# A transformer block with a mixture of experts on one core: the slots' first layer computed transposed, the routing weights from the tokens' side, eight groups in place of five, and another order of work at the start

## The chip, the cores and the metric

The kernel runs on one core of a Trainium2 chip. The metric is device time in microseconds (us) for one execution, as the median of several runs. TensorE is written PE (its weight loads PEld), VectorE DVE, ScalarE ACT, GpSimd POOL, SyncE SP.

## The reference

The input is `x`, 16 batches of 512 tokens with 128 features. Cut to what matters:

```
mod = silu(c) @ wmod                       # per batch: sa, ca, ga, sb, cb, gb
h = layernorm(x) * (1 + ca) + sa
x = x + ga * attention(h)                  # 16 heads of 8, rope, causal mask, softmax, proj
h = layernorm(x) * (1 + cb) + sb           # hidden state of a token
probs = sigmoid(h @ router_w.T + bias)     # 160 experts
top_w, top = top_k(probs, 8);  top_w = 2.5 * top_w / sum(top_w)
routed = sum over the 8 chosen e of top_w[e] * (silu(h @ w_gate[e].T) @ w_down[e].T)
shared = silu(h @ w_gate_shared.T) @ w_down_shared.T
out = x + gb * (routed + shared)
```

Each expert has 64 inner features, so two experts make a pair of 128, and there are 80 pairs. 8192 tokens with 8 choices each are 65536 rows to be sent through an expert.

## The kernel before, in words

**Two stages.** The attention stage goes through 16 batches times 4 groups of 4 heads, 64 passes of `attend(gg, pacer)`. The later stage, called the slots' stage below, sends the chosen rows through the experts. The order on PE, SP, ACT and DVE is written out by hand. A small clock in the program (`Steps`, `Pacer`) counts the modelled time of the matmuls issued so far and decides where background work is put between them; nothing of that clock exists at run time.

**Attention.** `prepare(b)` normalises a batch, and `rotate` and `values` make its queries, keys and values. Queries and keys go to DRAM (`parts`) and come back spread over 96 rows (`fetch`, tiles `qrep`, `krep`). `maxima` takes the row maxima of the scores on DVE, `shift` puts them into `qrep` through a DMA (`qrep<-mT`), `exponentials` runs on ACT, and `weighted` multiplies by the values. `project` adds the result to `x`. `route` then computes hidden states and the eight choices of a batch. Both run as background steps inside later passes.

**Groups, blocks, quads.** The batches are cut into `GROUPS = (4, 4, 4, 3, 1)`. When the last batch of a group is routed, `place(gr)` gives every chosen row a slot: slots are sorted by pair of experts, each pair takes whole blocks of 128 slots, at least one. A group of n batches is given 32n + 80 blocks, since up to 80 blocks can be partly full. Four blocks are a quad. The last 8 quads of a group (6 in a group of one batch) are spare: `spare_quads` holds their code under a runtime branch. The quads that always run are 44, 44, 44, 36 and 22, in sum 190.

**Scatter and gather.** POOL sends rows of hidden states to their slots with indirect DMAs (`scattering`, `xg<-hs,idx`, 128 rows each, 512 in all), a batch after its group is placed. Before that the slots are set to zero (`clear`, `xg<-zeros`, 256 KB each, from SP): after 5 of the 14 items of each attention pass one clear is issued, and what is left over is issued after the last pass. The rows of spare quads in `yg` are cleared in the same list. After a group's last quad POOL fetches the results (`gathering`, `got<-yg,idx`, 512 in all), eight for a block of 128 tokens, and `combine` adds the eight up on DVE, and scales them. `Pacer(PACE_SLOTS, scatter, gather)` with PACE_SLOTS = 0.9 places one indirect DMA per 0.9 us of modelled time, scatters first. `add_up(LAG)` with LAG = 4 keeps at most four fetched blocks waiting before DVE is told to combine one.

**A quad.** The loop over `i` runs one stage for each of several quads:

```
("load", i + 3), ("load_down", i - 3), ("name_up", i - 1), ("name_down", i - 5),
("end_weights", i - 4), ("begin_weights", i - 3),
("turn", i), ("up", i - 2), ("back", i - 4), ("down", i - 6),
```

`load` reads 512 slots' rows (`xs<-xg`, 256 KB), `load_down` the second layer's weights (`wd<-in_wdT`, 256 KB, address from a register). `turn` transposes the rows on PE (four 128x128 f32), and ACT copies them to `xT`. `up` multiplies with `xT` as the stationary operand and the pair's weights `wg[:, pid]` as the moving one, 130 columns: 128 for the two experts, and two router columns, from which DVE and ACT compute the slot's weight (`begin_weights`, `end_weights`, in pairs of quads). A bf16 matmul with `away` adds -1e30 where a slot belongs to the other expert of the pair. ACT applies silu (`su`). Because the slots now lie on partitions, `back` transposes again on PE, and DVE copies to `hwT`. `down` multiplies by `wd`, DVE scales by the weight into `y`, and SP stores it (`yg<-y`, 256 KB). `shared_expert(b)` computes the shared expert of a batch as background steps through one PSUM bank `o`.

**The start.** `modulation` and the bias parts are computed first, inside a scratch pool. Only then are the attention's pool and its constants made (`ident`, `wqk`, `turn`, ...). DVE clears the first pair of `qrep`/`krep`, POOL the others and the value tiles. All constants (`load_rest` too) are loaded before the first `prepare`, and the first pass waits in the program until batch 1 is prepared.

Of the kernel before, what the change touches and what calls it, by code (L numbers as in the profile page):

```python
# [9 lines left out]
FP = mybir.dt.float32  # L10
BF = mybir.dt.bfloat16
I32 = mybir.dt.int32
# [23 lines left out]
GROUPS = (4, 4, 4, 3, 1)  # L36
TOPK = 8
FAR = 1e30
TINY = 1e-30
LAG = 4  # L40

PACE, PACE_SLOTS = 1.3, 0.9
# [28 lines left out]
def block_kernel(ctx: ExitStack, tc: tile.TileContext, t: dict, out: bass.AP):  # L71
# [49 lines left out]
    fetch_x(0)  # L121
    with tc.tile_pool(name="pmod", bufs=1, space=PSUM) as pp, tc.tile_pool(
        name="smod", bufs=1
    ) as sp:
        mod = modulation(nc, t, const, pp, sp)
# [9 lines left out]

        bias3 = const.tile([3, E], BF, tag="bias3", name="bias3")
        three_ = sp.tile([1, 3, E], BF)
# [3 lines left out]
        nc.vector.tensor_tensor(three_[:, 2, :], bias_e, three_[:, 1, :], ALU.subtract)  # L141
        for i in range(3):
            nc.sync.dma_start(out=bias3[i : i + 1, :], in_=three_[:, i, :])
    attn = ExitStack()
    sa = attn.enter_context(tc.tile_pool(name="attn", bufs=1))
    now.ps = attn.enter_context(tc.tile_pool(name="attn_ps", bufs=1, space=PSUM))
    c = SimpleNamespace(
        ident=load("ident", [P, P]),
        wqk=load("wqk", [D, 2, 2, D], pool=sa),
        bqk=load("bqk", [D, 2, 2], pool=sa),  # L150
        turn=load("turn", [D, 2, S], pool=sa),
        wv=load("wvT", [D, D], pool=sa),
        identb=load("identb", [P, P], BF),
        mask_q=load("mask_q", [P, 2, P], BF, pool=sa),
        mask_k=load("mask_k", [P, 2, P], BF, pool=sa),
        wproj=wproj,
        onesb=load("onesb", [P, P], BF),
    )

    def load_rest():  # L160
        c.wrout = load("wroutT", [D, E])
        c.wgs = load("wgsT", [D, I])
        c.wds = load("wdsT", [I, D])
        c.bias_p = load("bias_p", [NC, 2])
        c.ones = load("ones", [P, 1])
        c.earlier = load("earlier", [P, P], BF)
        c.many = load("many", [1, P], BF)
        c.pairs = load("pairs", [NC, 2, NC])
        c.spread = load("spread", [NC, 2, E])
        c.table = load("table", [P, 2, NKM])  # L170

    eps = const.tile([P, 1], FP, tag="eps", name="eps")
    nc.vector.memset(eps, EPS)
    minus = const.tile([P, 1], FP, tag="minus", name="minus")
    nc.vector.memset(minus, -1.0)
    zeros = const.tile([P, 2, D], FP, tag="zeros", name="zeros")
    nc.vector.memset(zeros, 0.0)
# [6 lines left out]

    stat = const.tile([P, 2, NB * NBLK, 2], FP, tag="stat", name="stat")

    def moments(kind, b, blocks):
        for j in blocks:  # L190
            six = sb.tile([P, 6], FP, tag="six", name="six", bufs=2)
            vec.bn_stats(six, xs[b][:, j, :])
            vec.bn_aggr(stat[:, kind, b * NBLK + j, :], six)
# [46 lines left out]
    reps = []  # L240
    for i in range(NREP):
        pair = [
            sa.tile([P, GH, S], BF, tag=f"{side_}rep{i}", name=f"{side_}rep{i}") for side_ in "qk"
        ]
        for rep in pair:
            (in_order(nc.gpsimd.memset(rep, 0.0).ins) if i else nc.vector.memset(rep, 0.0))
        ones_ = pair[1][MROW : MROW + 3]
        (in_order(nc.gpsimd.memset(ones_, 1.0).ins) if i else nc.vector.memset(ones_, 1.0))
        reps.append(pair)

    vs = [sa.tile([P, NBLK, VW], FP, tag=f"v{i}", name=f"v{i}") for i in range(3)]
    for v in vs:
        in_order(nc.gpsimd.memset(v, 0.0).ins)
        in_order(nc.gpsimd.memset(heads_of(v)[:, :, :, HD : HD + 1], 1.0).ins)
# [5 lines left out]
    def prepare(b):  # L260

        for j in range(0, NBLK, 2):
            moments(0, b, (j, j + 1))
            yield
# [222 lines left out]
    rows = [tc.dram_tile([P, NBLK, D], FP, name=f"rows{b}") for b in range(NB)]  # L487

    somes = const.tile([1, len(GROUPS)], I32, tag="somes", name="somes")

    class Group:
        def __init__(self, g):
# [4 lines left out]
            self.scale = sb.tile([P, self.tb], FP, tag=f"scale{g}", name="scale")  # L497
            self.idx = sb.tile([P, self.tb, TOPK], I32, tag=f"idx{g}", name="idx")
            self.shift = sb.tile([P, self.nk, 2], FP, tag=f"shift{g}", name="shift")
            self.pid = sb.tile([1, self.nq, 9], I32, tag=f"pid{g}", name="pid")  # L500
            self.some = somes[:, g : g + 1]
            self.away = sb.tile(
                [P, -(-2 * self.nk // P), P], BF, tag=f"away{g}", name="away"
            )
            self.m, self.before = [], []
            self.xg = tc.dram_tile([self.nk * P, D], FP, name=f"xg{g}")
# [13 lines left out]
    def route(gr, i):  # L520
# [40 lines left out]
        yield  # L561

        top = sb.tile([P, NBLK, TOPK], FP, tag="top", name="top")
        for j in range(NBLK):
            vec.max(top[:, j, :], key[:, j, :])
            vec.match_replace(
                out=key[:, j, :], in_to_replace=top[:, j, :], in_values=key[:, j, :], imm_value=1.0
# [4 lines left out]
        vec.tensor_scalar(m, key, 0.0, None, ALU.is_gt)  # L572
# [13 lines left out]
        yield  # L586

        rs = gr.scale[:, i * NBLK : (i + 1) * NBLK]
        vec.reciprocal(top, top)
        vec.tensor_reduce(rs, top, AX.X, ALU.add, negate=True)  # L590
        vec.tensor_scalar(rs, rs, TOPK_EPS, None, ALU.add)
        vec.reciprocal(rs, rs)
        vec.tensor_scalar(rs, rs, ROUTED, None, ALU.mult)

    def place(gr):
# [41 lines left out]

# [58 lines left out]
        lim = gr.shift[:, :nk, :]  # L696
# [715 lines left out]
```

## Time and profile before

| | |
|---|---|
| median of 3 runs | 1918.97 us (1918.86 to 1922.9) |
| profiled execution, its own time | 1925.86 us |
| its span (first to last instruction) | 1924.1 us |
| busy: PE, DVE, ACT, POOL | 1584, 1254, 827, 1118 us |
| mean granted PE clock | 0.934 |
| moved by DMA | 377 MB, mean 196 GB/s |

In the profile a stretch of time ("window") is given with each engine's busy time, the granted PE clock and the DMA engines' busy share. A group line reads: line of the source, engine, operation, out<-in, count, then total busy and mean ns of one, then the idle time ahead of them and what ended it. An f32 matmul counts as two instructions here (two passes).

### The profile page before, as it was taken

What the parts mean: (1) busy time and instruction counts of PE and PEld (TensorE: products, weight loads), DVE (VectorE), ACT (ScalarE), POOL (GpSimd) and SP (SyncE); (2) the same over time, 40 slices, a digit from 0 to 9 for tenths busy, and PEclk for the clock granted to TensorE, in tenths of its full rate; (3) what the DMA queues carried; (4) which work ended last, traced back from release to release, by engine and by line L of the source; (5) the groups of instructions that cost most, each with busy time, mean ns of one, the idle gap of its engine ahead of it and who ended that gap; (6) DMA issues with size and microseconds to landing.
All of it is one profiled execution on the core that took longest, in us unless ns stands there. A gap on an engine that the chain in (4) does not pass through costs nothing. (4 is left out here: it accounts for less than half of the span.)

```text
span 1924.1 us, 38397 instructions
## 1 busy us (share of the span) xinstructions
PE 1584.2 (82%) x12683; PEld 1133.7 (59%) x12747; DVE 1253.8 (65%) x3325; ACT 826.6 (43%) x1366; POOL 1117.9 (58%) x1139
## 2 busy tenths in 40 slices
PE   2799999998999989999888887888898878878700
PEld 1355555554555545555468776777788777777600
DVE  2677888887788867787636554546576656666622
ACT  1366666655666556664544332333233323323100
POOL 4001111047775477845657476777777777777776
PEclk8799999998999999999999898999899989999855
DMA  2456555565676667843257676778688878878622
GB/s 83 105 175 201 170 174 170 163 197 177 191 234 188 199 192 219 262 127 117 77 185 244 197 251 203 240 246 275 214 266 272 258 225 272 255 251 254 196 58 57
DMA packets 246678, 377.03 MB, mean 196 GB/s; under 512 B 37604, under 2 KB 136261, under 8 KB 246469
## 3 DMA queue, kind: packets, MB, share of 16 engines
q1 hardware_dynamic: 213700, 307.17, 51.4%
q0 software_dynamic: 32768, 67.17, 12.1%
q8 instruction: 119, 1.95, 0.4%
q14 instruction: 91, 0.74, 0.1%
HBM read 195.15 MB, written 178.26 MB: 194 GB/s over the span
## 5 line engine op out<-in xcount | busy, mean ns | idle before, releaser
L741 POOL DMA_INDIRECT xg<-hs,idx x512 | 493.4, 964 | 284.5 <-issue 95.0
L950 POOL DMA_INDIRECT got<-yg,idx x512 | 491.5, 960 | 156.7 <-issue 123.5
L1212 DVE TENSOR_REDUCE mins<-s 128x2 f32<-128x1024 f32 (+3 forms) x448 | 395.9, 913 | 123.5 <-PE s L104 121.7
L1212 ACT ACTIVATE pT<-s 128x1024 f32<-128x1024 f32 x320 | 323.0, 1021 | 176.7 <-PE s L104 172.3
L104 PE MATMUL s<-wg,xT 128*128 x1520 | 279.6, 307 | 0.6 <-issue 0.6
L104 PEld LDWEIGHTS s<-wg,xT 128*128 128x128 f32 x1520 | 241.6, 200 | 11.3 <-issue 1.2
L111 PE MATMUL turn<-ident,xs 128*128 128x128 f32 x760 | 123.8, 287 | 121.8 <-issue 49.7
L104 PE MATMUL s<-krep,qrep 96*128 96x512 bf16 (+3 forms) x1024 | 197.8, 306 | 31.9 <-DMA qrep<-parts 19.0
L104 PE MATMUL down<-wd,hwT 128*128 x1520 | 206.6, 280 | 3.7 <-DVE y L1212 3.7
L235 POOL TENSOR_TENSOR rot<-rot,three 128x512 f32<-128x512 f32 x32 | 36.8, 1160 | 291.4 <-ACT three L1212 289.4
L104 PE MATMUL s<-qrep,krep 128*128 128x128 bf16 (+3 forms) x960 | 181.6, 299 | 25.3 <-DVE mins L1212 12.3
L104 PE MATMUL av<-pT,v 128*32 128x512 f32 (+3 forms) x2048 | 193.4, 449 | 0.0
L104 PEld LDWEIGHTS down<-wd,hwT 128*128 128x128 f32 x1520 | 190.8, 197 | 4.1 <-DVE y L1212 4.0
L1212 ACT COPY xT<-turn 128x512 f32<-128x512 f32 x190 | 109.8, 578 | 164.8 <-PE turn L111 161.8
L111 PEld LDWEIGHTS turn<-ident,xs 128*128 128x128 f32 x760 | 85.6, 145 | 156.8 <-issue 116.4
L1212 DVE TENSOR_TENSOR z<-s,shift 128x8 f32<-128x8 f32 x190 | 29.6, 156 | 219.3 <-PE s L104 206.5
L104 PEld LDWEIGHTS <-identb 128*128 128x128 bf16 x1280 | 122.0, 100 | 84.9 <-issue 7.0
L104 PE MATMUL s<-identb,away 128*128 128x128 bf16 (+1 forms) x760 | 171.2, 225 | 0.0
L1212 ACT ACTIVATE su<-s 128x512 f32<-128x512 f32 x190 | 113.6, 598 | 129.3 <-DVE z L1212 121.8
L1212 DVE COPY hwT<-back 128x512 f32<-128x512 f32 x190 | 131.0, 689 | 44.2 <-PE back L111 43.6
L1212 DVE TENSOR_TENSOR y<-down,w 128x512 f32<-128x512 f32 x190 | 131.2, 691 | 38.5 <-PE down L104 33.6
L104 PEld LDWEIGHTS <-qrep 96*128 96x128 bf16 x1024 | 83.6, 99 | 119.7 <-issue 95.5
(179 smaller groups left out, 2356.6 us busy)
## 6 DMA issues: line engine op xcount, KB each, us to landing
xg<-zeros SPq DMA_DIRECT2D x228, 256.0 KB
xs<-xg SPq DMA_DIRECT2D x190, 256.0 KB
wd<-in_wdT SPq DMA_DIRECT2D x190, 256.0 KB
yg<-y SPq DMA_DIRECT2D x190, 256.0 KB
krep<-parts SPq DMA_DIRECT2D x64, 288.0 KB
qrep<-parts SPq DMA_DIRECT2D x192, 96.0 KB
parts<-three SPq DMA_DIRECT2D x96, 128.0 KB
yg<-zeros SPq DMA_DIRECT2D x38, 256.0 KB
```

The source lines that it names most:

```text
L104: steps.last = nc.tensor.matmul(out_, lhsT=lhsT, rhs=rhs, start=start, stop=stop).ins
L111: steps.last = nc.tensor.transpose(out_, in_, ident).ins
L235: in_order(getattr(nc.gpsimd, op)(*args).ins)
L741: s = nc.gpsimd.indirect_dma_start(out=gr.xg, out_offset=bass.IndirectOffsetOnAxis(ap=gr.idx[:, NBLK * i + j, k : k + 1], axis=0), in_=h[: ...
L950: s = nc.gpsimd.indirect_dma_start(out=got[:, k, :], out_offset=None, in_=gr.yg, in_offset=bass.IndirectOffsetOnAxis(ap=gr.idx[:, NBLK * i ...
L1212: return getattr(self.engine, op)(*args, **kwargs)
```

## The change

- `GROUPS = (2, 3, 3, 2, 2, 2, 1, 1)`, LAG = 3, PACE_SLOTS = 0.75. The quads that always run are 28, 36, 36, 28, 28, 28, 22 and 22, in sum 228; the blocks to clear rise from 228 quads plus 38 spare ones to 288 plus 60.
- `up` is transposed: the pair's weights are stationary. Since these are chosen at run time, ACT and DVE copy two of the four blocks each from `wg` to a fixed tile `wq` (`fetch_up`, addresses read into registers of ACT and DVE). The result has the inner features on partitions, so `back` and the copy `hwT` go away, and silu's output feeds `down`.
- The mask (`away`, four bf16 matmuls a quad) becomes one bf16 matmul of two rows, `half` by `hide`. `hide` is made in `place`, goes to DRAM, and is loaded for two quads at once (`load_hide`).
- The slot's weight is no longer computed. ACT copies the second layer's result to `y` unscaled. `route` stores the keys and the mask of choices of each batch to DRAM (`keys`, `chosen`), a new background step `weights(b)` loads them in the slots' stage and picks the eight weights of each token in slot order, and `combine` multiplies the eight rows by them.
- The quad's pipeline is two stages shorter. PSUM gets two buffers each for `turn` and `up`, and one pair of banks `s`.
- At the start the moments of batch 0 come first on DVE, `load_first` loads what `prepare(0)` needs right behind `wmod`, POOL clears the tiles (two pairs first, the rest behind `prepare(0)`), `load_rest` comes after the first four fetches, and the first pass no longer waits for batch 1.

```diff
-GROUPS = (4, 4, 4, 3, 1)
+GROUPS = (2, 3, 3, 2, 2, 2, 1, 1)
-LAG = 4
+LAG = 3
-PACE, PACE_SLOTS = 1.3, 0.9
+PACE, PACE_SLOTS = 1.3, 0.75
...
+    moments(0, 0, range(NBLK))
...
+        mod = modulation(nc, t, const, pp, sp, load_first)
...
+    clear_v(0)
+    clear_rep(0)
+    clear_rep(1)
...
+        nc.sync.dma_start(out=keys[b], in_=key)
...
+        nc.sync.dma_start(out=chosen[b], in_=m)
...
+            hide = sb.tile([P, P], BF, tag="hide", name="hide", bufs=2)
+            vec.tensor_copy(hide[:k], pa[:k, n * P : (n + 1) * P])
+            for a in range(2):
+                nc.sync.dma_start(
+                    out=gr.hide[a, c0 * I : (c0 + k) * I].rearrange("(n s) -> n s", s=P),
+                    in_=hide[a:k:2],
+                )
...
+        def load_hide(self):
+            if self.q % 2 == 0:
+                two = moe.sb.tile([2, 2, S], BF, tag="hides", name="hides", bufs=3)
+                at = slice(4 * P * self.q, 4 * P * (self.q + 2))
+                nc.sync.dma_start(
+                    out=two, in_=self.gr.hide[:, at].rearrange("a (n s) -> a n s", s=S)
+                )
+                self.hide, self.other.hide = two[:, 0, :], two[:, 1, :]
...
+        def fetch_up(self):
+            self.wq = self.tile([P, 4, P], "wq", 3)
+            for engine, copy, at in (
+                (mybir.EngineType.Activation, act.copy, 0),
+                (mybir.EngineType.DVE, vec.tensor_copy, 2),
+            ):
+                for j, pid in enumerate(self.numbers(engine, 1 + at, 2, NC - 1), at):
+                    copy(
+                        self.wq[:, j, :], wg[:, bass.ds(pid, 1), :].rearrange("p o n -> p (o n)")
+                    )
...
         def up(self):
-            pu = bank2().rearrange("p a (j n) -> p (a j) n", j=2)
+            pu = now.ps.tile([P, S], FP, tag="up", name="up", bufs=2)
             for j in range(4):
+                to = pu[:, j * P : (j + 1) * P]
                 mm(
-                    pu[:, j, 0 : P + 2],
+                    to,
+                    self.wq[:, j, :],
                     self.xT[:, j * P : (j + 1) * P],
-                    wg[:, bass.ds(self.pids[j], 1), :].rearrange("p o n -> p (o n)"),
...
+            mm(pu, c.half, self.hide, False, True)
+            self.u = self.tile([P, S], "su", 3)
+            act.activation(self.u, pu, AF.Silu)
...
-        def back(self):
-            pt = now.ps.tile([P, S], FP, tag="back", name="back")
-            for j in range(4):
-                turned(pt[:, j * P : (j + 1) * P], self.u[:, j, :], c.ident)
-            self.hT = self.tile([P, S], "hwT", 3)
-            vec.tensor_copy(self.hT, pt)
...
-                    self.hT[:, j * P : (j + 1) * P],
+                    self.u[:, j * P : (j + 1) * P],
...
-            vec.tensor_tensor(
-                y,
-                py.rearrange("p (n d) -> p n d", d=D),
-                self.w[:, self.q % 2].unsqueeze(2).broadcast_to([P, 4, D]),
-                ALU.mult,
-            )
+            act.copy(y.rearrange("p n d -> p (n d)"), py)
...
+    def weights(b):
+        while len(weighed) < weighing.index(b):
+            yield
+        key = moe.sb.tile([P, NBLK, E], FP, tag="wkey", name="wkey")
+        nc.sync.dma_start(out=key, in_=keys[b])
+        m = moe.sb.tile([P, NBLK, E], BF, tag="wm", name="wm")
+        nc.sync.dma_start(out=m, in_=chosen[b])
+        yield LATER
+        base = moe.sb.tile([P, NBLK, E], FP, tag="base", name="base")
+        vec.tensor_tensor(base, m, c.high.unsqueeze(1).broadcast_to([P, NBLK, E]), ALU.mult)
...
+        for n, (by, mask) in enumerate(((16, 0x7FFF), (0, 0xFFFF))):
+            vec.tensor_scalar(digit, bits, by, mask, ALU.logical_shift_right, ALU.bitwise_and)
+            vec.tensor_tensor(both, base, digit, ALU.add)
+            yield
+            for j in range(NBLK):
+                vec.max(eight[:, n, j, :], both[:, j, :])
...
+        vec.tensor_tensor(
+            got, got, w[:, j, :].unsqueeze(2).broadcast_to([P, TOPK, D]), ALU.mult
+        )
         for n in (4, 2, 1):
...
     for i in range(-3, len(quads) + 5):
+            ("load_hide", i),
+            ("load_down", i - 1),
+            ("fetch_up", i),
...
+            ("name_down", i - 3),
+            ("down", i - 4),
```

## The prediction

> **What bounds the kernel now.** I read the page's slices, then busy time by windows set at the stages' borders. The windows' columns: length, busy PE, PEld, DVE, ACT, POOL (instructions), granted PE clock, DMA share, GB/s.
>
> ```profile
> PE   2799999998999989999888887888898878878700
> POOL 4001111047775477845657476777777777777776
> DMA  2456555565676667843257676778688878878622
> ```
> ```profile
> 0.00:77.00 77.00, 31.15 (x113) 17.41 (x114) 29.57 (x76) 12.71 (x24) 23.13 (x23) 0.80 0.31 79
> 77.00:972.00 895.00, 841.59 (x6809) 468.50 (x6871) 695.51 (x1693) 540.61 (x792) 408.48 (x403) 0.98 0.59 177
> 972.00:1260.00 288.00, 239.10 (x1940) 216.43 (x1941) 150.91 (x499) 99.17 (x192) 188.35 (x196) 0.94 0.71 225
> 1260.00:1816.00 556.00, 467.27 (x3812) 428.55 (x3810) 351.74 (x998) 172.93 (x358) 421.90 (x439) 0.96 0.81 253
> 1816.00:1924.00 108.00, 5.12 (x14) 2.78 (x14) 26.08 (x63) 1.18 (x2) 76.06 (x81) 0.50 0.24 62
> ```
>
> A start of 77 us with PE 40% busy; attention to 972 us, PE 94% busy; the quads' loop from the first `turn` at 974 to 1816 us, 842 us or 4.43 for each of 190 quads, PE 84% busy, DMA 0.71 to 0.81; a tail of 108 us with POOL alone. From 1260 us POOL's 439 instructions in 556 us are one per 1.27 us, an indirect DMA (0.96) and its gap (0.30): POOL is full to the end.
>
> ```profile
> L741 POOL DMA_INDIRECT xg<-hs,idx x512 | 493.4, 964 | 284.5 <-issue 95.0
> L950 POOL DMA_INDIRECT got<-yg,idx x512 | 491.5, 960 | 156.7 <-issue 123.5
> ```
>
> One undisturbed quad in PE's timeline (start, length):
>
> ```profile
> 1597.99 0.66 PE L111 MATMUL turn<-ident,xs 128*128 128x128 f32 x4 [0.97 <-ACT xT L1212]
> 1598.49 0.39 PE L104 MATMUL s<-wg,xT 128*128 x2
> ...
> 1599.77 0.61 PE L111 MATMUL back<-ident,su 128*128 128x128 f32 x4
> 1600.22 1.06 PE L104 MATMUL down<-wd,hwT 128*128 x8
> 1601.11 0.60 PE L111 MATMUL turn<-ident,xs 128*128 128x128 f32 x4
> ```
>
> From start to start: `turn` 0.50, `up` with masks 1.28, `back` 0.45, `down` 0.89, in sum 3.12 us. The rest of 4.43 is the shared expert, the clock (0.95), waits for `xs` and the groups' ends, where PE branches over the spare code:
>
> ```profile
> L896 PEldq COMPARE_BRANCH  x5: 3787/5002/5340, 1185.7 to 1814.5; - x5
> ```
>
> **The start: -10 us (-18 to -3).** Batch 0's statistics waited behind tile clears, though `cT`, loaded after `x`, was there at 3.9 us:
>
> ```profile
> 19.36 0.29 DVE L1212 BATCH_NORM_STATS2 six<-x 128x6 f32<-128x128 f32 x1
> ```
>
> After the change they come first, and the next bound on DVE is the modulation and bias work, which ended at 12.5 us. ACT's normalisation then starts near 13 instead of 21.9: 9 us. POOL's clears ahead of its first subtraction are two pairs and one value tile, 6 x 1.80 + 0.87 = 12 us, done before they are needed; the other two pairs stand behind that subtraction (near 29 us), and end before 45, about when their fetch is reached. The first pass stood at 77.1 us behind batch 1's 9 us of matmuls (68.2 to 77.1). Without that wait it starts earlier, but those matmuls move into a stage that is 94% PE, so I count 1 us.
>
> **Attention: +5 us (0 to +14).** Eight placings instead of five; by 972 us about 5.6 are done instead of 2.6. One costs PE some 4.5 us (the 160-column f32 matmuls 1.2, four of 0.3 over the blocks, transposes 0.7, the rest small). Three are 13.5 us, against 53 us in which PE idles here. `hide` goes through SP with two buffers and three pieces, so DVE's third copy waits for the first piece's stores, 2 to 3 us a group, and the `maxima` queue behind it; three score buffers cover most. The routing's five weight steps go.
>
> **Clears: +8 us (0 to +18).** 64 passes issue 320 of 348 clears. With the last passes' own, 35 stand in a row on SP between the last `qrep<-mT` (957 us before) and the first `xs`: 35 x 262 KB is 9.2 MB, 29 us at the highest rate that I found:
>
> ```profile
> 1140.00:1150.00 10.00, 7.96 (x73) 7.57 (x72) 4.20 (x13) 2.91 (x7) 7.63 (x8) 1.00 0.99 322
> ```
>
> The remaining attention covers 14 us. Of the other 15 some return, since the first three `turn`s of before took 5.6 us to come.
>
> **The quads' loop: +3 us (-65 to +75).** 228 quads, 38 more. By the reference's choices for these inputs no spare quad runs, before or after. The floor of each engine:
> - PE: 0.50 + 0.89 (`up` now has `down`'s shape) + 0.25 for the mask (one bf16 pass of 512 columns; an f32 one of two passes is 0.62) + 0.89 = 2.53 us. 228 x 2.53 = 577; the shared expert 16 x 3.3 = 53; placings 15; by clock 0.95: 679. Seven groups' ends inside the loop (four before) at 6.5 us, 4.3 idle and the rest at a lowered clock: 45. Floor 724, with 2% for what I overlook 740.
> - ACT: `xT` 0.58, `su` 0.60, `y` 0.58, two copies like `gate` 0.27, and a register load, on ACT 0.28 to 0.76 in the branch's rows, 0.48: 2.8 us, 635.
> - DVE loses `hwT`, `y` and the weight steps (2.0 us a quad), and gets two copies (below 0.30, the 128x128 addition) and a load of 0.31, 0.9 x 228 = 205; the product over 128x1024, twice the 0.68 of 128x512 less its fixed part, 1.25 x 64 = 80; `weights`, 0.83 + 2 x (0.51 + 0.83) + 8 x 0.32 + 10 x 0.2 = 8 us x 16 = 131. Little more than before, and `wq` is asked for two quads ahead.
> - POOL: in program order 370 scatters come before the loop (314 before), and 485 gathers are placed within it (453). Gathers begin after 28 quads, some 105 us; then 64 scatters and 480 gathers at 1.255 us take 683: 788.
> - DMA: before, 288 us at 225 and 556 at 253 GB/s are 205 MB. Added: 38 quads x 0.786 = 30 MB, keys and choices 8, gathers 3, scatters -4, `hides` 1: 244 MB. A share of 0.81 at 253 and 0.71 at 225 means 315 GB/s when full: 775 us.
>
> So the longest floor passes from PE to DMA. Lookahead is three quads, as before, so a late transfer is mostly met by others already queued; I take 3% loss, 800 us. Add 31 for seven groups' ends, in which SP stands 4.5 us, and 15 for the stretch of quads 64 to 128: there 96 gathers are placed in 22 quads, 120 us of POOL against 78 of quads; LAG 3 lets POOL be 24 gathers, 30 us, behind, so 12 are left, once or twice. DVE then waits for `got`, behind it `wq`'s copies, and PE for those. Sum 845. The low end is PE's 740 with 37 of waits, the high end is the first rival.
>
> A row speaks against the new DVE copies: POOL's DMAs take 0.94, but one of those that ran beside DVE's additions took 0.2 more.
>
> ```profile
> 1801.51 1.47 DVE L1212 TENSOR_TENSOR got<-got 128x512 f32<-128x512 f32 x3
> 1802.33 1.14 POOL L950 DMA_INDIRECT got<-yg,idx  x1 [0.30 <-issue]
> ```
>
> Its mean over all is 0.96, so I add nothing. [...]
>
> **The tail: -55 us (-62 to -45).** 81 POOL instructions follow 1816 us, because gathers trail the quads. After the change the group before the last is fetched while the last one's 22 quads run, so 32 remain: 32 x 1.255 = 40, before it `y`, its landing and the branch 5, after it landing 2.6, combining 1.25 + 2.1, the store 2.5: 53.
>
> **Sum.** -10 + 5 + 8 + 3 - 55 = -49. The profiled execution took 1925.86 us (span 1924.1), so its like would take 1877; the median of the runs is 6.9 lower, so 1870.
>
> **The rivals.**
> - DMA becomes the bound and stays below its peak. For: the best 25 us windows of before reach 280 and 284 GB/s; 10 us at 322 is short. Against: in those windows PE was 92 to 95% busy and DMA not asked for more. At 284: 244 MB take 859 us, with 31 + 27 for groups' ends and waits 917, +75: 1870 + 72, about 1942. It decides when the rate between groups' ends falls under some 289 GB/s (a loop of 894 us). Chance 0.24.
> - DMA hides, and PE's floor rules: a loop of 777 us, 1870 - 68 = 1802, but POOL's 788 and the 40 us of tail hold it near 1815. For: without gathers a quad needs 0.88 MB, 2.8 us. Against: gathers run beside most quads. Chance 0.14.
> - The copies only change their engine: each register load stands open on ACT for 1.0 us, PE's median for such loads, and `y` and `xT` queue behind it. 3.4 us a quad with waits of 0.3 are 844, with 31 + 15: 890, +45: 1912. For: ACT's order is fixed. Against: on PE these loads delayed hardly a matmul. Chance 0.11.
>
> **How the numbers follow.** The forecast (1840 to 1900) has 0.51. 0.2%, 4 us, is about what a measurement of this kernel can tell from no change. Faster: 0.51 + 0.14 and more than half of the ACT case, 0.72; same 0.04; slower 0.24. For 8 in 10 the range takes most of the fast case and half of the slow one's upper side: 1820 to 1947.
>
> **What would show it.** Right: the first `six` near 4 us and the first pass near 60; DMA's share at 0.9 or more in the loop; a quad at 3.7 us; fewer than 40 gathers after the last `down`. Wrong: a loop with DMA still at 0.8 while ACT or DVE hold PE up, POOL's DMA above 1.0 us in the mean, or DVE waiting for `got` in the loop by more than 40 us.

## The result, and the profile after

The changed kernel takes 2000.76 us in the median of four runs (1994.59 to 2006.29), the kernel before 1918.91 on the same chip: a ratio of 1.042, 95% interval 1.039 to 1.046. The forecast was 1870 us with a range of 1820 to 1947. The kernel became slower instead of faster, and slower than the slowest rival said (1942).

The profiled execution has a span of 1998.5 us, 74.4 more than before. First the same three rows of its page (40 slices), then busy time by windows at the new borders of the stages, with the columns of before.

```profile
PE   3799998999899988889959788887777789888880
POOL 5101117713775567775726757677777774757736
DMA  3365646756766676767688688887787888888871
```
```profile
60.00:1002.00 942.00, 860.70 (x6933) 471.94 (x6931) 703.44 (x1693) 544.04 (x798) 463.72 (x458) 0.98 0.64 197
1002.00:1024.00 22.00, 0.27 (x2) 0.30 (x3) 1.10 (x7) 1.08 (x3) 0.96 (x1) 0.56 1.02 331
1024.00:1945.00 921.00, 768.74 (x5227) 644.02 (x5225) 440.86 (x1358) 526.03 (x1212) 628.52 (x625) 0.90 0.82 265
1945.00:1998.50 53.50, 0.22 (x2) 0.02 (x1) 14.86 (x29) 0.59 (x1) 30.24 (x32) 0.52 0.21 59
```

Attention now ends at 1002 us instead of 971. Then TensorE stands for 22 us while the DMA engines are full (a share of 1.02, 331 GB/s) with the clears left over. The loop of 228 quads takes 921 us, 79 more than that of 190, at a granted clock of 0.90 (0.94 to 0.96 before) and a DMA share of 0.82. The tail is 53.5 us instead of 108. So the change adds 31 us by attention's end, the start included, then 19 and 79, and takes 55 off the tail: 74 us more.

GpSimd's two groups, to be set beside those of before, and an undisturbed stretch of TensorE's timeline (start, length):

```profile
L968 POOL DMA_INDIRECT got<-yg,idx x512 | 514.6, 1005 | 240.0 <-issue 120.3 <-SPq L868 45.7 <-PE turn L110 22.1
L746 POOL DMA_INDIRECT xg<-hs,idx x512 | 499.0, 975 | 325.5 <-PE s L103 124.8 <-issue 92.2 <-PE turn L110 26.2
```
```profile
1928.07 0.60 PE L110 MATMUL turn<-ident,xs 128*128 128x128 f32 x4
1928.50 1.06 PE L103 MATMUL up<-xT,wq 128*128 128x128 f32 x8
1929.49 0.39 PE L103 MATMUL up<-hides,half 2*128 2x512 bf16 x1
1929.81 1.16 PE L103 MATMUL down<-wd,su 128*128 x8
1930.80 0.60 PE L110 MATMUL turn<-ident,xs 128*128 128x128 f32 x4
```

From one `turn` to the next are 2.73 us: `turn` 0.43, `up` 0.99, the masks 0.32, `down` 0.99. That is the quad of the change, 0.4 us under the 3.12 of before. But the mean over the loop is 921 / 228 = 4.04 us. The difference stands in single waits of several microseconds. Those of the loop, on TensorE and VectorE (total, times, longest):

```profile
PE o L110 <- DMA hr<-rows: 33.1, 7, 6.7
PE up L103 <- DVE wq L1227: 28.0, 14, 6.0
PE up L103 <- DMA hides<-hide: 24.2, 13, 2.9
DVE got L1227 <- DMA got<-yg,idx: 64.8, 22, 5.7
```

One such place in full, from the timelines of TensorE, VectorE, SyncE and GpSimd:

```profile
1425.15 1.23 PE L103 MATMUL up<-xT,wq 128*128 128x128 f32 x4 [3.67 <-DVE wq L1227]
1428.24 0.58 PE L103 MATMUL up<-hides,half 2*128 2x512 bf16 x1 [1.87 <-DMA hides<-hide]
1420.97 1.23 DVE L1227 TENSOR_TENSOR got<-got,w 128x1024 f32<-128x1024 f32 x1 [2.86 <-DMA got<-yg,idx]
1424.40 0.39 SPq L992 DMA_DIRECT2D out<-xr  x1
1425.39 0.33 SPq L800 DMA_DIRECT2D hides<-hide  x1
1422.15 0.95 POOL L968 DMA_INDIRECT got<-yg,idx  x1 [0.30 <-issue]
1423.40 0.94 POOL L968 DMA_INDIRECT got<-yg,idx  x1 [0.30 <-issue]
```

VectorE waits for gathered rows, sums them to 1424.4, and only then copies two weights of the next quad: TensorE has waited 3.67 us for them. The output's store waits for that sum too, and the masks' load stands behind the store in SyncE's order, so TensorE waits again. Beside all this GpSimd issues one gather per 1.25 us, without a break.

### The profile page after: what moved, and what is told of

The parts are those of the page before. It is cut to its first block, busy times and chain, and to the rows that moved or that the text cites. A ratio compares the mean times of both kernels' runs of the same rounds, so it can differ in the third digit from the quotient of the medians.

```text
span 1998.5 us, 39212 instructions
## 1 busy us (share of the span) xinstructions
PE 1652.7 (83%) x12248; PEld 1129.4 (57%) x12248; DVE 1185.2 (59%) x3150; ACT 1081.0 (54%) x2031; POOL 1151.8 (58%) x1142
## 3 DMA queue, kind: packets, MB, share of 16 engines
q1 hardware_dynamic: 265152, 375.32, 58.6%
## 5 line engine op out<-in xcount | busy, mean ns | idle before, releaser
L968 POOL DMA_INDIRECT got<-yg,idx x512 | 514.6, 1005 | 240.0 <-issue 120.3
L103 PE MATMUL down<-wd,su 128*128 x1824 | 279.7, 299 | 33.9 <-ACT su L1227 9.7
L103 PEld LDWEIGHTS down<-wd,su 128*128 128x128 f32 x1824 | 235.3, 202 | 116.4 <-issue 47.4
L103 PE MATMUL up<-xT,wq 128*128 128x128 f32 x1824 | 267.0, 292 | 34.2 <-DVE wq L1227 28.0
L103 PEld LDWEIGHTS up<-xT,wq 128*128 128x128 f32 x1824 | 245.2, 208 | 37.7 <-DVE wq L1227 30.9
L1227 DVE COPY wq<-wg 128x128 f32 x456 | 89.9, 244 | 243.9 <-PE up L103 163.7
L1227 ACT COPY y<-down 128x512 f32<-128x512 f32 x228 | 133.9, 587 | 182.9 <-PE down L103 126.4
L103 PE MATMUL s<-qrep,krep 128*128 128x512 bf16 (+3 forms) x1024 | 195.2, 303 | 32.6 <-DMA qrep<-mT 12.0
L1227 ACT ACTIVATE su<-up 128x512 f32<-128x512 f32 x228 | 136.4, 598 | 103.7 <-PE up L103 102.8
L1227 DVE TENSOR_TENSOR got<-got,w 128x1024 f32<-128x1024 f32 x64 | 78.3, 1223 | 102.1 <-DMA got<-yg,idx 99.0
L1227 ACT COPY wq<-wg 128x128 f32 x456 | 113.6, 296 | 42.3 <-issue 12.5
```

The source lines that it names most:

```text
L103: steps.last = nc.tensor.matmul(out_, lhsT=lhsT, rhs=rhs, start=start, stop=stop).ins
L968: s = nc.gpsimd.indirect_dma_start(out=got[:, k, :], out_offset=None, in_=gr.yg, in_offset=bass.IndirectOffsetOnAxis(ap=gr.idx[:, NBLK * i ...
L1227: return getattr(self.engine, op)(*args, **kwargs)
```

## The experiments

The experiments ran on chips that differ. On one, in this document the slower chip, the kernel before takes some 2200 us (the sets that begin with a_groups5, a_again and b_nogot); on the others, the faster chips, some 1920. Each ratio is to the kernel before on the same chip. The one trace of the kernel before is of a faster chip.

**Groups, quad, DMA volume, early loads (the slower chip, 2198 us).** Theory A says that the eight groups cost the time, B that the transposed quad's new waits do.

a_groups5: the change with the groups of before.
```
-GROUPS = (2, 3, 3, 2, 2, 2, 1, 1)
+GROUPS = (4, 4, 4, 3, 1)
```


> The changed kernel with the five groups of before, (4, 4, 4, 3, 1): 190 quads instead of 228, five placings, 266 clears; everything else as changed. Theory 1, the number of groups is the price: attention ends near 972 us again instead of 1002 (three placings fewer before that), the first turn follows within 3 us instead of 22 (no clears left over), the loop falls from 921 us to about 770 with its 38 quads gone, the tail grows from 53 to about 100 us because gathers trail again: in sum about 1850 us. Theory 2, the new quad is the price (copies of the weights on ACT and DVE, DVE stuck behind gathered rows): the loop stays at 4.4 us a quad or more as in before, some 840 us, and the whole at 1920 us or above.

b_groups8: the kernel before with the eight groups (and one buffer for `mT`, to make room).
```
-GROUPS = (4, 4, 4, 3, 1)
+GROUPS = (2, 3, 3, 2, 2, 2, 1, 1)
```


> The kernel before with the eight groups (2, 3, 3, 2, 2, 2, 1, 1) alone (and one buffer instead of two for the tile mT, for space): 228 quads of the old kind. Theory 1, the number of groups is the price: attention +30 us, clears +18, 38 quads more at 4.4 us +165, tail -55: near 2075 us, above the changed kernel. Theory 2, the new quad is the price: the eight groups alone cost little because gathers start earlier and the tail is short, 1880 to 1930 us.

a_halfwd: an odd quad uses the down weights of its even neighbour, 114 loads fewer.
```
+            if self.q % 2 and not self.alone:
+                self.wd = self.other.wd
+                return
```


> The changed kernel, but every odd quad uses the second layer's weights that the even quad loaded (wrong weights for the odd quads): 114 loads of 256 KB fewer, 30 MB, nothing else. Theory D, the loop is bound by DMA: at 270 GB/s 30 MB are 110 us, the loop falls from 921 to about 815 and the whole to about 1890 us. Theory W, the loop is bound by waits of the in-order engines (gathered rows, shared expert, groups' ends): less than 25 us, 1975 us or more.

a_early: masks loaded two quads earlier, `hr` used 8 modelled us after its load instead of at once.
```
-            ("load_hide", i),
+            ("load_hide", i + 2),
...
+        yield 8.0
```


> The changed kernel with the masks' load (hides) two quads earlier and eight modelled us between the load of the shared expert's rows (hr) and the first step that uses the program's time for it; no work is added or removed. Theory W: PE waits 24 us for hides and 33 us for hr in the loop, most of it returns: -40 us, about 1960. Theory D, DMA-bound: the time is only moved, within 10 us of 2000.

Measured: 1.012 (1.008 to 1.017), 1.072 (1.069 to 1.075), 1.068 (1.065 to 1.071) and 1.072 (1.069 to 1.074). With the eight groups alone (and one `mT`, whose own price was not tried) the kernel before is as slow as the changed kernel of the next set (1.073). Attention ends at 1051 us with five groups and at 1079 to 1097 with eight, and the first `turn` follows 3 or 20 to 21 us later. Leaving out 30 MB of weights is worth 0.4% against a_early, so the volume of DMA isn't what binds on this chip, where its share in the loop is 0.65 in a_early and 0.58 without those loads (0.82 in the changed kernel on the faster chip). The loads moved ahead bring nothing against 1.073.

**Waits of the quad (the slower chip, 2214 us).** a_again is the changed kernel itself, a_groups5b is a_groups5 once more.

> The changed kernel as it is, once more, so that the other runs of this call have its time and its trace on their own chip. Both theories: 1.035 to 1.075 of the time before. If the chip is the slow one of the first experiments, the span divides as in the run with early loads: attention's end near 1095, first turn near 1115, the loop of quads near 1190, tail near 55.

> The changed kernel with the groups of before (4, 4, 4, 3, 1): 190 quads for 228, 28 clears fewer left over, fewer placings inside attention. Theory A (the eight groups make the loss; the transposed quad itself is free): 0.94 to 0.955 of the changed kernel, of which attention 30 to 45 us, leftover clears 15 to 20 us, and the loop 80 to 100 us. Theory B (the quad's new waits make it, the groups little): at most 2% less than the changed kernel, all of it ahead of the loop.

a_allact: all four weight copies on ScalarE.
```
-                (mybir.EngineType.DVE, vec.tensor_copy, 2),
...
-                for j, pid in enumerate(self.numbers(engine, 1 + at, 2, NC - 1), at):
+                for j, pid in enumerate(self.numbers(engine, 1 + at, 4, NC - 1), at):
```


> The changed kernel with all four weight copies of a quad on ScalarE and none on VectorE: a copy can no longer stand behind VectorE's wait for gathered rows, and VectorE has 456 copies fewer, by 244 ns 111 us less work. Theory B (the copies behind VectorE's waits hold TensorE up): the loop loses the 28 us of TensorE's wait for VectorE's copies and half of the lumps in the stretch of gathers, 30 to 60 us in all. Theory A: ScalarE gains 456 copies of 296 ns, 135 us, and stays under TensorE in the loop, so 0 to 20 us either way. If VectorE's copies slowed GpSimd's gathers, their mean falls from 1005 to near 960 ns.

a_y3: a third `y` (and two buffers for the masks' rows, for three, to make room).
```
-            y = self.tile([P, 4, D], "y", 2)
+            y = self.tile([P, 4, D], "y", 3)
```


> The changed kernel with three buffers for y in place of two (the space comes from the third buffer of the masks' rows). Theory B (ScalarE waits 47 us for y's store, and TensorE behind it): the wait is all but gone, and the loop is 20 to 45 us shorter. Theory A: the wait goes, and the time shows up in another wait of the same quads; within 10 us.

Measured: 1.073 (1.066 to 1.080), 1.018 (1.012 to 1.023), 1.085 (1.081 to 1.089), 1.077 (1.073 to 1.082). So groups are worth 5% here, and both cures of single waits are at best nothing. But they were made for the waits of the faster chip, and on this one TensorE idles elsewhere. Ahead of `down` it is 265 us in the loop of a_again, where it was 34 on the faster chip; ahead of the masks 15 instead of 24, ahead of the other matmuls of `up` 23 instead of 34, ahead of all that use the bank `o`, with `hr` among them, 10 instead of 36. Here are `down`'s rows of a_again and a_allact:

```profile
L103 PE MATMUL down<-wd,su 128*128 x1824 | 313.6, 324 | 264.7 <-issue 145.0
L103 PE MATMUL down<-wd,su 128*128 x1824 | 318.5, 327 | 279.1 <-ACT y L1226 224.6
```

The waits put down to ScalarE's `y` grow from 119 to 225 us, but the idle time ahead of `down` as a whole only from 265 to 279, as much as in a_y3, and that without a named cause ("issue") falls from 145 to 50. Causes are named from updates of semaphores, and a_again's profile holds 24603 of them where the changed kernel's on the faster chip holds 49508. So these runs do not show that ScalarE became a bound, and a_early, a_allact and a_y3 do not tell what their cures are worth on the faster chip.

**Less work for TensorE, less for GpSimd, fewer groups (a faster chip, 1920 us).** Theory C: the denser quad lowers the clock that TensorE is granted.

b_groups4 and a_groups4: four groups in both kernels (a_groups4 also with two buffers for the masks' rows).
```
+GROUPS = (5, 5, 4, 2)
```


> The kernel before with four groups (5, 5, 4, 2): 176 quads for 190, one placing and 14 clears of slots fewer, but the last group's two batches leave 64 gathers for the end instead of 32. Theory A (each group costs some 12.7 quads, its end, its placing in attention and its clears): 14 quads by 4.4 us, 62 us, and some 15 us of attention and group's end go, 0 to 40 us come back in the tail; 0.95 to 0.985 of the time before. Theory B (what the groups cost is hidden, TensorE's quads are not the bound): within 1% of the time before.

> The changed kernel with four groups (5, 5, 4, 2), and two buffers of masks' rows for three so that it fits. Theory A: it follows the kernel before with four groups within 2%, that is 0.955 to 1.0 of the time before, since the transposed quad itself neither costs nor gains. Theory C (the transposed quad runs TensorE more densely, and the granted clock takes back what the fewer matmuls give): in the loop the granted clock is lower by 0.05 or more than in the kernel before with the same groups, and the loop's time is the same or longer.

a_noturn: no transposes in a quad.
```
-            for j in range(4):
-                turned(pt[:, j * P : (j + 1) * P], self.xs[:, j, :], c.ident)
-            act.copy(self.xT, pt)
+            act.copy(self.xT, self.xs.rearrange("p n d -> p (n d)"))
```


> The changed kernel without the four transposes of a quad (ScalarE copies the rows as they are into the same tile: the products are of untransposed rows, all else is kept): TensorE has 912 of its matmuls of 273 ns fewer, 0.45 us a quad, 100 us of the loop at full clock. Theory C (the loop is paced by TensorE at the clock that it is granted): the loop is 90 to 150 us shorter, and the granted clock in the loop is up by 0.03 or more. Theory B (waits for gathers, stores and DMA latency pace it): the loop is 0 to 50 us shorter, and the clock hardly moves.

a_nogot: half of the gathers, and with them half of VectorE's products and sums.
```
-            for k in range(TOPK):
+            for k in range(TOPK // 2):
```


> The changed kernel with four of a token's eight gathers and half of the sums that go with them (the other four experts' rows are left out): GpSimd has 256 gathers of 1.0 us fewer, VectorE's products and sums are half as long. Theory B (VectorE stands in the loop behind gathers, and its weight copies behind that): the waits of VectorE for gathered rows all but go, and the loop is 60 to 110 us shorter. Theory C: the loop is 0 to 40 us shorter, and the tail some 20 us shorter in either theory.

Measured: b_groups4 1.001 (0.998 to 1.004), a_groups4 1.017 (1.013 to 1.020), a_noturn 1.029 (1.026 to 1.032), a_nogot 1.026 (1.023 to 1.029), the changed kernel itself 1.042. 14 quads fewer shorten the loop of the kernel before from 842 to 769 us, and the time stays: the tail grows from 108 to 181. Theory A missed this; the other reading, that TensorE's quads are not the bound of the kernel before, had said within 1%. a_groups4 shows the signs of C, a clock of 0.85 in the loop and a loop of 845 us. But a_noturn speaks against C: TensorE loses 912 matmuls and the loop only 27 us (921 to 894), while the clock falls to 0.87 instead of rising. And a_nogot speaks against B: without 256 gathers, 320 us of GpSimd's queue and 17 MB, the loop is 11 us shorter and the time 30. The loops of the two:

```profile
1026.00:1920.00 894.00, 702.91 (x4315) 571.15 (x4315) 443.19 (x1361) 522.31 (x1212) 623.77 (x625) 0.87 0.84 273
1028.00:1938.00 910.00, 761.65 (x5227) 631.88 (x5227) 365.79 (x1303) 525.62 (x1212) 376.74 (x385) 0.90 0.78 251
```

In a_noturn TensorE's busy time falls by 66 us and its idle time rises from 152 to 191. No theory with one bound fits both runs.

**GpSimd's queue or `xr`'s buffers (a faster chip, 1923 us).** The change took `xr` from four buffers to three; in a_groups4 TensorE stood for 130 us in eleven waits for `hr`, and in the one followed in SyncE's timeline the loads of `xr` and `hr` came 5.7 us after the store of an output, for which the freed buffer of `xr` waits. Theory X: that is the loss. Theory G: indirect DMAs back to back set the end.

a_xr4 (eight groups) and a_g5xr4 (five, (4, 4, 4, 3, 1)):
```
-                two = moe.sb.tile([2, 2, S], BF, tag="hides", name="hides", bufs=3)
+                two = moe.sb.tile([2, 2, S], BF, tag="hides", name="hides", bufs=2)
...
-        xr = moe.sb.tile([P, NBLK, D], FP, tag="xr", name="xr", bufs=3)
+        xr = moe.sb.tile([P, NBLK, D], FP, tag="xr", name="xr", bufs=4)
```


> The changed kernel (eight groups) with four buffers for xr as before the change, and two for the masks' rows to make room. Theory X: TensorE's waits for hr (33 us, and 35 us of weight loads beside them) all but go, the granted clock in the loop rises from 0.90 towards 0.93, and the loop is 30 to 60 us shorter: 0.97 to 0.985 of the changed kernel. Theory G: with eight groups GpSimd idles 136 us in the loop, so it doesn't hold this gain back; if another wait takes the place of hr's, within 1% of the changed kernel.

> The same four buffers for xr with the groups of before (4, 4, 4, 3, 1). Some 708 indirect DMAs are left when attention ends, as in the kernel before: at 1.25 us they take 885 us. Theory G: attention's end near 965, and the end not before 965 + 885 + 20 to 45 us of idle = 1870 to 1895 us, a ratio to the kernel before of 0.975 to 0.99. Theory X alone (no bound from GpSimd): 190 quads of 3.4 us and a tail of 60 us, 965 + 650 + 60 = 1675 to 1750 us.

a_g5smooth, on top of a_g5xr4:
```
+        yield 8.0
...
+        if b - 1 in stored and j == 1:
+            store(b - 1)
```


> As the run with five groups and four xr, and besides the store of an output waits until the next batch's second sum, and hr's use comes 8 steps after its load: fewer of SyncE's and TensorE's waits. Theory G: the same time within 0.7%, since GpSimd's indirect DMAs set it. Theory X: 10 to 40 us less than with the four buffers alone.

a_g33343, on top of that:
```
+GROUPS = (3, 3, 3, 4, 3)
```


> As the run before it, with the groups (3, 3, 3, 4, 3): 188 quads, and the first slots are placed one batch earlier, so that some 340 rows' scatters instead of 315 are out when attention ends; 683 indirect DMAs are left, 854 us. Theory G: 25 to 40 us less than with (4, 4, 4, 3, 1), 0.955 to 0.98 of the kernel before. Theory X: no difference but the tail's, which grows by some 60 us with the last group's 96 gathers.

Measured: 1.039 (1.036 to 1.043), 1.017 (1.013 to 1.020), 1.010 (1.006 to 1.013), 1.020 (1.017 to 1.024). X falls as the main cause: with four `xr`, `hr`'s waits are still 33.1 us at eight groups, where the time is that of the changed kernel, and 89 us at five. For a_g5xr4 (span 1955 us) G is nearer, where X says 1675 to 1750; its own range of 1870 to 1895 was missed by 60 us, since GpSimd's idle time was 75 us and not 20 to 45. Smoothing (a_g5smooth) took `hr`'s waits away and gave 15 us back, 0.8%: inside X's 10 to 40 us and just outside G's 0.7%. Meanwhile TensorE's waits for VectorE's weight copies grew from 53 to 101 us, which stand behind 172 us of VectorE's waits for gathered rows. The last run, for which G said 0.955 to 0.98, was to start its scatters earlier; in its trace no more of them lie ahead of the loop (316, and 317 in a_g5smooth), and the gain that hung on them isn't there.

a_xr4 and a_g5xr4 differ in their groups alone. So on this chip the groups are worth 42 us (1999.76 to 1957.45), and the other 34 of the 76 us above the kernel before stay with five groups. Which part of the change makes these was not isolated.

The account that G makes, from the traces of the faster chips: the indirect DMAs that begin after the first `turn`, at the median distance of 1.25 us, and what longer distances (over 1.6 us) add. That such a sum comes near the last gather is bookkeeping; what tells kernels apart is how small the idle time is.

| kernel | loop from, us | DMAs left | x 1.25 us | added idle, us | sum, us | last gather begins, us |
|---|---|---|---|---|---|---|
| before | 974 | 709 | 886 | 40 | 1900 | 1916 |
| b_groups4 | 972 | 727 | 909 | 17 | 1898 | 1913 |
| a_groups4 | 964 | 729 | 911 | 43 | 1918 | 1936 |
| a_g5xr4 | 971 | 707 | 884 | 75 | 1930 | 1945 |
| a_g5smooth | 967 | 707 | 884 | 56 | 1907 | 1922 |
| a_g33343 | 981 | 708 | 885 | 70 | 1936 | 1950 |
| changed | 1024 | 653 | 816 | 136 | 1976 | 1989 |

In all rows the sum lies 13 to 18 us below the last gather, and the kernel ends 9 to 10 us after it. With four or five groups GpSimd's queue idles for 17 to 75 us of some 950. With eight it has 136 us: 56 DMAs fewer are left, but the loop begins 50 us later, and at small groups the gathers run out and wait for quads. In the changed kernel's timeline:

```profile
1669.61 0.94 POOL L968 DMA_INDIRECT got<-yg,idx  x1 [0.30 <-PE up L103]
1689.00 1.63 POOL L968 DMA_INDIRECT got<-yg,idx  x1 [18.44 <-PE turn L110]
```

**The same half of the gathers left out of the five-group forms (the slower chip, 2215 us).** This shortens GpSimd's queue by 320 us, as it was done for eight groups. a_g5nogot has the four `xr` of a_g5xr4.

> The kernel before with four of a token's eight gathers and the sums of those four alone (the other four experts' rows are left out): 256 indirect DMAs of 1.25 us fewer, 320 us off GpSimd's queue. Theory G (that queue sets the end of the kernel before): the tail falls from 108 to some 30 us and the loop loses what VectorE waited for gathers, 75 to 135 us in all, 0.93 to 0.96. Theory H (the chain of quads sets the end, as with eight groups): 20 to 60 us, the tail alone, 0.97 to 0.99.

> The changed kernel with five groups (4, 4, 4, 3, 1) and four xr, and the same half of the gathers left out. Theory G: the loop falls from 874 us to 190 quads of 3.3 to 3.9 us, 630 to 740 us, and the time to 0.86 to 0.93 of the kernel before, more below the run with all gathers than the kernel before without half is below its own. Theory H: 20 to 60 us less than with all gathers, 0.985 to 1.01.

Measured: b_nogot 0.932 (0.928 to 0.935), a_g5nogot 0.933 (0.929 to 0.936). The kernel before gains 6.8%, as G says, and four times what the changed kernel gained with eight groups (1.6%, on a faster chip). The five-group form falls to 0.933 from 1.012 (a_groups5) and 1.018 (a_groups5b), both with three `xr`. But it was to pass the kernel before, and only draws level: there the loop of transposed quads takes 967 us from first to last `y`, that of before 938, and half of the quads come at 2.8 us or less and a quarter at 6.8 or more.

This chip can't test a full queue, though. With all gathers GpSimd has 259 us (a_groups5) and 285 us (a_groups5b) of added idle time there, counted as in the table. For the kernel before an estimate is some 240 us: b_nogot's first `turn` comes at 1069 us, and of the 1136 from there to the last gather of a run of 2215 us, 709 DMAs at 1.25 us take 886. So the gathers, or the sums and the 17 MB that go with them, hold the end up on this chip too, but not by filling the queue; in the five-group form TensorE's idle time ahead of `down` falls from 286 us (a_groups5b) to 153 without half of them. That GpSimd's queue sets the end of the kernel before rests on the faster chips: on its 40 us of idle time, and on b_groups4, where 73 us off the loop left the time as it was. For the five-group form of the change it is argued from the table. That the transposed quad pays once GpSimd is out of the way is not shown.

No version here that fetches all rows beats the kernel before: b_groups4 equals it, the next is a_g5smooth, 1% slower.

## Why the prediction was wrong

**Start: -10 said, about -1 measured.** The steps came as said: the first `six` at 3.71 us, the first pass at 60.1 instead of 77.1. But the first two passes, now with batch 1's matmuls among them, take 49.5 us instead of 36, 10 of it work of TensorE; then 2 to 4 us of lead are left, and after pass 13, into which the first placing falls, both kernels are near 267 us. "I count 1 us" for work that goes into a stage 94% full was the wrong term.

**Attention: +5 said, +31 with the start.** Up to attention's end TensorE is busy for 883 us instead of 872 and idle for 20 us more. By then five placings are done and the sixth is begun, against three before, so some two and a half more and not three. Their work came about as priced, 4.5 us each, but none of it was hidden, and the waits that came with them were priced too low. The 53 us of idle that were to hide it were no cover. a_xr4 and a_g5xr4, which differ in groups alone, end attention at 1004 and 969 us: 35 us, some 14 for each placing more. Which of a placing's steps makes the waits was not tried.

**Clears: +8 (0 to +18) said, +19.** The row of 35 clears came as said, 28.2 us on SyncE, and at the rate said (331 GB/s, share 1.02, in the 22 us after the last pass). Attention covered 11 us of it and not 14, the first loads of `xs` then took 4 us more to bring a `turn`, and none of it came back.

**Loop: +3 said, +79; the step that failed most.** The sum said that the longest floor passes from TensorE to the DMA engines, took their 775 us as the floor and added waits. The volume was right, 921 us at 265 GB/s being 244 MB, but the engines were 0.82 busy, a_noturn's loop drew 273 GB/s, and 17 MB less in a_nogot took off 11 us. The engine with the longest busy time stayed TensorE, and its own row was sized too small: 2.53 us a quad for a measured 2.73 at full clock (`up` and `down` 0.99 each for 0.89, the masks 0.32 for 0.25), 46 us over 228 quads; and 0.95 for the clock, which was 0.90. In the trace 129 of the loop's 769 busy microseconds fall into stretches at half clock, 65 of 706 before. There the matmuls of `up` and `down` start 0.21 us apart, at full clock 0.11, so some half of the difference, 32 us, is lost by it. So TensorE was busy for 769 us where the sum had 679, and idle for 152 where it left 166; that makes the 76 us by which the loop missed 845. That the idle time fits is luck in part: the 31 us for seven groups' ends did not come (TensorE's seven branches over spare code in the loop took 7 us in sum, 4.1 at most, where before one took 3.8 to 5.3), and other waits came in their place. TensorE's work alone is not the pace either, since a_noturn's 66 us less of it gave 27.

**Tail: -55 said, -55 measured.** 32 gathers follow the last `down`, 53.5 us.

**GpSimd: the term that was missing.** The prediction read "POOL is full to the end" from the profile and then used it only as a floor of one loop, 788 us, and of a tail. It is one queue from attention's end to the end of the kernel: loop and tail trade gathers, so -55 in the tail is no gain by itself, as b_groups4 shows. Seen so, the kernel before had 40 us of slack there, and the eight groups paid 50 us at the loop's start for 56 DMAs fewer, 70 us; with 38 quads more the queue's idle time grew by 96. The changed kernel has left that bound: neither 912 matmuls fewer nor 256 gathers fewer bring more than 30 us. That its chain of quads is the next bound is argued from this, and which wait in it counts stays open.

**Rivals.** The DMA rival was nearest in time (1942), and its sign came, a rate under 289 GB/s (269 from 1160 us on). Its mechanism is not what the runs show, as said above. Its 284 GB/s was no top either: from 1413 to 1438 us the kernel before moved 297. "PE's floor rules" gave the loop 777 us in all, where TensorE was busy for 769 and idle for 152 more. The copies on ScalarE were no bound of their own as built: ScalarE was busy for 526 of the loop's 921 us. Of the signs for "wrong", two appeared, a DMA share of 0.8 with other engines holding TensorE and 64.8 us of VectorE's waits for `got`; of the third, the mean DMA of GpSimd, half: 1005 ns for gathers, 975 for scatters.

**The weight copies and the gathers.** With 456 weight copies on VectorE the mean gather took 1005 ns, 960 in the kernel before: 23 us over 512. On the slower chip it took 1000 ns in a_again and 979 in a_allact, without these copies: 11 us over 512, and the kernel got slower (1.085, a_again 1.073). So the loss that can go with the copies is small; a_nogot, which has them too, has 974. That the copies themselves made the gathers longer was not shown.

## What to carry to other kernels

An engine that is full in two neighbouring stages is one account across both: add up all that is left in its queue from the first stage's start, and count a shorter tail as a gain only if that sum falls. A change of tiling that relieves such a queue has to be charged with everything that its finer grain repeats, here placings, clears and quads, at the rate of the stage they land in. Before a cure is judged, look whether the wait that it is for stands in the trace of the chip on which it is tried: three cures here moved nothing on a chip where those waits were smaller and another wait, ahead of `down`, was eight times as long as where they had been read.

## What the runs showed of the hardware

In the two kernels with four groups TensorE's granted clock was lower where TensorE idled more, and not where it worked more: in the loop after 1260 us it was 0.97 with TensorE 84% busy in b_groups4, and 0.81 at 67% in a_groups4. Here are the slices of a_groups4's page, then both windows, b_groups4 first, and the eleven waits for `hr` of a_groups4's loop:

```profile
PE   3799999999989999979897898886756666566200
PEclk8899999999999999989998898987878888778655
```
```profile
1260.00:1741.00 481.00, 405.82 (x3348) 371.48 (x3346) 307.52 (x872) 151.28 (x313) 364.89 (x382) 0.97 0.82 256
1260.00:1809.00 549.00, 367.94 (x2324) 304.74 (x2324) 295.63 (x793) 233.61 (x537) 421.61 (x419) 0.81 0.71 224
PE o L110 <- DMA hr<-rows: 129.5, 11, 16.2
```

In a_groups4's timeline TensorE's first work after one long wait ran slower. Behind this wait of 15.5 us `turn` takes 1.06 us and `up` 1.92, some five microseconds later 0.66 and 1.06:

```profile
1578.53 1.09 PE L110 MATMUL o<-ident,hr 128*128 128x128 f32 x4 [15.52 <-DMA hr<-rows]
1579.41 1.06 PE L110 MATMUL turn<-ident,xs 128*128 128x128 f32 x4
1580.26 1.92 PE L103 MATMUL up<-xT,wq 128*128 128x128 f32 x8
1584.80 0.66 PE L110 MATMUL turn<-ident,xs 128*128 128x128 f32 x4
1585.30 1.06 PE L103 MATMUL up<-xT,wq 128*128 128x128 f32 x8
```

In the changed kernel's trace, as in that of the kernel before, the granted clock is either full or half. Each of the seven pauses of more than 5 us in the changed kernel's loop has a stretch of 6.8 to 10.2 us at half clock, which begins 1.5 to 4.3 us into the pause and ends 3.2 to 8.8 us after it. Such pauses are not the only places: 25 stretches at half clock, of 3.4 to 13.7 us, begin in that loop. Before, the loop idled for 136 us and had 82 at half clock; after, 152 and 182, with the idle time in longer pieces (13 us in pauses over 5 us before, 44 after).

On the slower chip the DMA packets of the changed kernel took about as long as on the faster (in the mean 71.5 ns in a_again and 70.7 over the 265152 packets of its largest queue), but the granted clock in the changed kernel's loop was 0.81 instead of 0.90, and TensorE idled there for 336 us instead of 152. Why stays open, so its stage times are compared only among themselves.
